# A four-layer convolution network on one core: the lead-in before the first matmul rebuilt

**Chip, cores, metric.** One core of a Trainium2 chip (trn2). The metric is device time in microseconds (us) of one execution, from the runs of one kernel on one chip; all runs quoted here are in the fast state (with one core no slower state showed: the granted clocks of the profiled runs lie between 0.952 and 0.955). Engines: PE (TensorE), DVE (VectorE), ACT (ScalarE), POOL (GpSimd), SP (SyncE, which issues most transfers).

## The reference

Four residual layers on x of 8192 samples x 8 channels x 16 x 16, float32. Each adds a layer of the group-normalized activations:

```python
x = x + L0(_gn(x))   # tensor-train matvec, cores of rank [1, 8, 8, 1], sizes [8, 16, 16], plus bias
x = x + L1(_gn(x))   # 3x3 convolution, batch norm over the whole batch, relu
x = x + L2(_gn(x))   # 3x3 convolution of values and weights quantized to +-127 (maximum over everything)
x = x + L3(_gn(x))   # 3x3 convolution with binarized weights, edge padding
```

`_gn` subtracts the mean and multiplies by 1/sqrt(var + eps) of each of four groups of channels of each sample. Batch norm and the global maximum force three passes over the 64 tiles of 128 samples (1 MiB each): pass 1 does layer 0 and the convolution of layer 1; pass 2 the batch norm and the maximum; pass 3 layers 2 and 3.

## The kernel before

First the constants, in program order (cut; every `by_channel` is 8 small transfers issued by SP):

```python
core2 = ...; for k in range(8): nc.sync.dma_start(core2[k * W:(k + 1) * W, k % 2], c2)
c0x = by_channel(c0, R * C, "c0x", setup)
for m0 in range(C): nc.sync.dma_start(c1x[m0 * H:(m0 + 1) * H], c1)
for r in range(R):                       # product of the first two cores, on DVE
    nc.vector.tensor_tensor(tmp, a, b, ALU.mult)          # 128x1024
    nc.vector.tensor_tensor(c01v, c01v, tmp, ALU.add)     # 128x1024, from r = 1
band1 = band(by_channel(w1, ...)); band2 = ...; band3 = ...   # five 128x384 operations each, DVE
# ... selectors, and kps = a small PE product for layer 3's correction
```

Then tiles 0 and 1 are loaded and normalized one after the other, and only then the main loop starts:

```python
for t in range(min(2, NT)):
    load_b(t); load_t(t); add_bias(t)         # xb: a copy in another layout, for the statistics
    norm_b_square(t)                          # ACT
    norm_b_sums(t)                            # DVE, four 128x1024 reductions
    norm_b_stats(t)                           # PE matmul into stb; DVE; POOL: power -0.5 of 64 columns
    norm_b_copy(t)                            # ACT: the power back into stb
    norm_b_apply(t)                           # DVE: xn = (xb - stb) * stb
expand(0, 0, 0); expand(0, 0, 1)              # PE pu, ACT copies it to u
for t in range(NT + 2):
    for q in range(NQ):                       # quarters of a tile
        # steps at r = 0..7, between the eight matmuls of main(t, q):
        at(2, ..., expand, next quarter, 0); at(6, ..., expand, next quarter, 1)
        # q == 0: at(4, norm_b_square, t + 2)
        # q == 1: at(0, norm_b_sums, t + 2);  at(7, norm_b_stats, t + 2)
        # q == 3: at(5, norm_b_copy, t + 2);  at(5, norm_b_apply, t + 2)
        main(t, q, steps)                     # PE: po, 8 matmuls of core01 with u (16 passes)
        conv_at(n, conv1)                     # PE: pc, an earlier tile
```

The PSUM tile `stb` has one buffer. Within an engine's stream the order of the program counts: in the kernel before, ACT's first copy of u (93.27 us) came only behind tile 1's copy into stb (93.11), though the pu that it reads had run at 81.52.

## Time and profile before

| | kernel before |
|---|---|
| median (range) of the runs beside the changed kernel | 4810.09 us (4809.37 to 4810.17, 4 runs) |
| span of the profiled run, granted clock | 4808.3 us, 0.955 |
| first po (the first matmul of the main work) | 99.26 us |
| end of pass 1 (SP issues the first load of pass 2) | 3217.39 us |
| PE busy | 92% |

Two marks carry the argument: the start of the first po, before which nothing of the main work is done, and the first load of pass 2, which SP issues when pass 1 is done.

### The profile page before, as it was taken

The numbers are of one execution on the slowest core, as the hardware profiler recorded it, in microseconds if no ns is written. First come the engines' busy times: TensorE is split into PE (matmuls) and PEld (weight loads), VectorE is DVE, ScalarE is ACT, GpSimd is POOL, SyncE is SP. The second block draws the span as 40 slices with busy tenths as digits, with TensorE's granted clock in tenths as the row PEclk, the third lists the DMA queues.
The fourth block names the chain that finished last, engine by engine and source line by source line (L and its number), as shares of the span: only waits on it lengthen the run. The fifth ranks groups of instructions, "written<-read, shape, count | busy, mean of one in ns | idle before, by whom it ended". The sixth has DMA issues, their size and how long they took to land. (4 is left out here: it accounts for less than half of the span.)

```text
span 4808.3 us, 47928 instructions
## 1 busy us (share of the span) xinstructions
PE 4409.3 (92%) x19338; PEld 1989.7 (41%) x19338; DVE 2689.6 (56%) x4058; ACT 2192.8 (46%) x1537; POOL 2009.3 (42%) x657
## 2 busy tenths in 40 slices
PE   2999999999999999999999999975555599999999
PEld 1444444444444444444444444431111244444444
DVE  4555555555555555545455555438888555665665
ACT  1444444444444444444444444434444455555553
POOL 3333333333332323242424232216666455556564
PEclk9999999999999999999999999986666799999999
DMA  2222221212222222222222222139997033333321
GB/s 90 79 79 97 79 97 75 101 70 100 76 95 81 89 87 88 88 88 88 88 88 88 88 88 79 53 138 398 382 383 307 18 140 131 132 140 132 132 104 79
DMA packets 82669, 581.16 MB, mean 121 GB/s; under 512 B 11536, under 2 KB 11664, under 8 KB 12048
## 3 DMA queue, kind: packets, MB, share of 16 engines
q1 hardware_dynamic: 82448, 578.10, 31.5%
q8 instruction: 153, 2.51, 0.2%
q14 instruction: 68, 0.56, 0.0%
HBM read 323.25 MB, written 254.80 MB: 120 GB/s over the span
## 5 line engine op out<-in xcount | busy, mean ns | idle before, releaser
L41 PE MATMUL po<-u,core 128*128 128x512 f32 x4096 | 1963.8, 607 | 2.2 <-ACT u L41 2.0
L41 ACT COPY u<-pu 128x2048 f32<-128x2048 f32 x512 | 955.8, 1867 | 1088.2 <-PE pu L41 1088.2
L41 PEld LDWEIGHTS po<-u,core 128*128 128x128 f32 x4096 | 721.6, 190 | 809.7 <-issue 802.9
L41 POOL TENSOR_TENSOR mv<-mv,mhalf 128x4 f32<-128x4 f32 x128 | 130.7, 1021 | 1790.5 <-DVE mv L41 1790.5
L41 POOL TENSOR_TENSOR mvb<-mvb,mhalf 128x64 f32<-128x64 f32 x64 | 675.1, 10549 | 164.7 <-DVE mvb L41 164.7
L41 PE MATMUL pc<-x1n,band 128*128 128x480 f32 (+1 forms) x1536 | 677.7, 578 | 4.0 <-DVE x1n L41 4.0
L41 PE MATMUL pf<-t,band 128*128 128x512 f32 x1536 | 676.0, 596 | 0.0
L41 PE MATMUL pu<-core,xn 32*128 32x256 f32 x8192 | 589.4, 402 | 11.6 <-ACT u L41 11.6
L41 PEld LDWEIGHTS pu<-core,xn 32*128 32x128 f32 x8192 | 371.3, 185 | 411.6 <-issue 386.7
L41 DVE BATCH_NORM_STATS2 bst<-y 128x6 f32<-128x512 f32 x256 | 177.7, 694 | 633.8 <-ACT y L41 633.8
L41 ACT ACTIVATE sq<-x 128x2048 f32<-128x2048 f32 x192 | 366.2, 1907 | 266.8 <-POOL x L41 266.1
L41 ACT ACTIVATE y<-pc,b 128x512 f32<-128x512 f32 x256 | 176.2, 688 | 663.0 <-PE pc L41 663.0
L41 PEld LDWEIGHTS pf<-t,band 128*128 128x128 f32 x1536 | 285.2, 189 | 390.6 <-issue 390.6
L41 DVE TENSOR_TENSOR x<-po,x 128x512 f32<-128x512 f32 x256 | 176.6, 690 | 482.5 <-PE po L41 240.4
L41 PEld LDWEIGHTS pc<-x1n,band 128*128 128x128 f32 x1536 | 293.3, 191 | 359.2 <-issue 359.2
L41 POOL TENSOR_TENSOR x<-x,z 128x1024 f32<-128x1024 f32 x128 | 299.8, 2365 | 185.2 <-ACT z L41 185.2
L41 POOL TENSOR_TENSOR x<-x,bias_t 128x2048 f32<-128x2048 f32 x64 | 289.4, 4521 | 181.7 <-DMA x<-in_xt 170.4
L41 POOL TENSOR_TENSOR x<-x,c 128x2048 f32<-128x2048 f32 x64 | 235.8, 3685 | 232.9 <-DVE t L41 221.9
L41 POOL TENSOR_TENSOR x<-x,yl 128x2048 f32<-128x2048 f32 x64 | 290.4, 4538 | 10.7 <-DMA x<-x_d 10.3
L41 PE MATMUL gb<-rows_c,sel 128*128 128x128 f32 x256 | 72.7, 436 | 237.3 <-DVE rows_c L41 237.3
L41 DVE TENSOR_TENSOR xn<-xb,stb 128x1024 f32<-128x1024 f32 x128 | 150.6, 1218 | 239.0 <-ACT stb L41 239.0
L41 DVE TENSOR_TENSOR x<-pf,x 128x1024 f32<-128x1024 f32 x128 | 156.4, 1222 | 116.1 <-PE pf L41 111.9
(161 smaller groups left out, 4027.7 us busy)
## 6 DMA issues: line engine op xcount, KB each, us to landing
x_d<-x SPq DMA_DIRECT2D x115, 1024.0 KB, 5.8
x<-x_d SPq DMA_DIRECT2D x115, 1024.0 KB, 8.3
xb<-in_xb SPq DMA_DIRECT2D x64, 1024.0 KB, 4.9
x<-in_xt SPq DMA_DIRECT2D x64, 1024.0 KB, 4.8
y_d<-y SPq DMA_DIRECT2D x64, 1024.0 KB, 3.8
yl<-y_d SPq DMA_DIRECT2D x64, 1024.0 KB, 11.4
out_dram<-x SPq DMA_DIRECT2D x64, 1024.0 KB, 3.9
c1x<-in_c SPq DMA_DIRECT2D x8, 64.0 KB, 2.2
```

Of the source, the lines that this page charges most:

```text
L41: return self.tc.keep_in_program_order(op(*args, **kwargs))
```

## The change

The intent is to start the main loop as early as tile 0 allows. The weights come in two transfers packed on the host, the product of the first two cores is done on PE, tile 0's power, copy and normalization go by quarters, tile 1's normalization moves into tile 0's main loop, and the other constants are built in slices between the first quarters. To make room, u has 2 buffers instead of 3 and yl of pass 2 has 4 instead of 5.

```diff
+PACK0 = [("c0", R * C), ("c1", R * H), ("core2", 2 * R * W), ("bias0", W)]
+PACK1 = [("w1", 9 * C), ("linb", C), ... ("w3all", C * C * 9), ("bias3", 1)]
+    w0 = load_pack(pack0, PACK0, const, "w0")          # one transfer on ACT's queue
+    def late_constants(late):                          # a generator: band1, band2, band3, selectors ...
+        w = load_pack(pack1, PACK1, late, "w1")
+        yield "load"
+        ...                                            # six more slices of DVE work, each with a yield
-        up = s.enter_context(tc.tile_pool(name="up", bufs=3))
+        up = s.enter_context(tc.tile_pool(name="up", bufs=2))
-            pool.tensor_tensor(mv[:, 1], mv[:, 1], mhalf[:, :NB], ALU.pow)
+            n = NB // NQ if by_quarter else NB
+            for a in range(0, NB, n):
+                pool.tensor_tensor(mv[:, 1, a:a + n], mv[:, 1, a:a + n], mhalf[:, :n], ALU.pow)
-        for t in range(min(2, NT)):
-            load_b(t) ... norm_b_apply(t)
-        expand(0, 0, 0)
-        expand(0, 0, 1)
+        for t in range(min(3, NT)):
+            load_b(t)
+            load_t(t)
+        rest = late_constants(...)
+        next(rest)
+        dve.tensor_tensor(c0x, w0["c0"]..., shz..., ALU.mult)
+        for n in range(C):
+            pe.matmul(cps[:, n], c0x[:, n]..., w0["c1"], start=True, stop=True)
+        norm_b_square(0)
+        ...  act.copy(core01, cps) in two halves
+        norm_b_sums(0)
+        norm_b_stats(0, by_quarter=True)
+        for q in range(NQ):
+            norm_b_copy(0, q)
+            norm_b_apply(0, q)
+            if q == 0:
+                expand(0, 0, 0)
+                expand(0, 0, 1)
+                add_bias(0)
         for t in range(NT + 2):
             for q in range(NQ):
+                if n > 0:
+                    next(rest, None)                   # one slice of constants
+                if t == 0 and NT > 1:
+                    if q == 0:
+                        at(0, True, norm_b_square, 1)
+                        at(0, True, norm_b_sums, 1)
+                        at(7, True, norm_b_stats, 1)
+                    elif q == 1:
+                        at(5, True, add_bias, 1)
+                        at(5, True, norm_b_copy, 1)
+                        at(5, True, norm_b_apply, 1)
+                        at(5, NT > 2, add_bias, 2)
-    with tc.tile_pool(name="p2", bufs=5) as p2, ...
+    with tc.tile_pool(name="p2", bufs=4) as p2, ...    # and kps moves here
```

## The prediction

> **What bounds the kernel now.** I read the page first, its row of PE over the span in 40 slices, then the stages with the windows view. In the windows rows the columns are the stretch and its length, then busy time and count of PE, PEld, DVE, ACT and POOL, the granted clock, the DMA share and GB/s.
>
> ```profile
> PE   2999999999999999999999999975555599999999
> 0.00:47.95 47.95, 1.65 (x6) 1.35 (x6) 31.89 (x71) 0.00 (x0) 1.75 (x15) 1.00 0.14 28
> 47.95:99.26 51.31, 5.68 (x37) 3.45 (x37) 20.26 (x23) 9.13 (x7) 34.64 (x5) 1.00 0.46 179
> 99.26:3214.00 3114.74, 3105.19 (x14302) 1452.36 (x14302) 1588.42 (x1965) 1363.17 (x954) 1020.31 (x251) 1.00 0.22 84
> 3214.00:3775.00 561.00, 291.09 (x1285) 95.24 (x1286) 446.36 (x854) 253.74 (x130) 354.39 (x130) 0.65 0.86 336
> 3775.00:4808.00 1033.00, 1005.67 (x3710) 437.30 (x3708) 602.63 (x1146) 566.76 (x446) 598.22 (x256) 0.99 0.31 117
> ```
>
> From 99.26 to 3214 us PE is busy 3105 of 3115 us, so layers 0 and 1 end when PE has done its work: whatever lets PE begin earlier moves everything after it by as much, and whatever makes PE wait there costs its full length. Before 99.26 PE does almost nothing. That lead-in is 2.1% of the time and the only place where the change can gain. Its chain stands in the timeline (start, length, then the instructions; in brackets the idle time before them and what ended it):
>
> ```profile
> 47.95 0.35 SPq L290 DMA_DIRECT2D xb<-in_xb  x1
> 52.94 2.35 DVE L41 TENSOR_REDUCE sumb<-xb 128x32 f32<-128x1024 f32 x2 [4.70 <-DMA xb<-in_xb]
> 60.70 10.57 POOL L41 TENSOR_TENSOR mvb<-mvb,mhalf 128x64 f32<-128x64 f32 x1 [0.48 <-DVE mvb L41]
> 82.52 10.56 POOL L41 TENSOR_TENSOR mvb<-mvb,mhalf 128x64 f32<-128x64 f32 x1 [6.74 <-DVE mvb L41]
> 93.27 1.86 ACT L41 COPY u<-pu 128x2048 f32<-128x2048 f32 x1
> 99.26 3.78 PE L41 MATMUL po<-u,core 128*128 128x512 f32 x4 [1.99 <-ACT u L41]
> 104.93 3.70 PE L41 MATMUL po<-u,core 128*128 128x512 f32 x8
> 120.35 0.38 PE L41 MATMUL stb<-sumb,sum 128*128 128x128 f32 x2
> 3198.59 12.86 PE L41 MATMUL pc<-x1n,band 128*128 128x512 f32 x24 [4.01 <-DVE x1n L41]
> ```
>
> Three parts: 48 us of constants before the first tile is even requested (some 90 small transfers issued by SP, core products on DVE); 5 us for the tile; then 46 us in which tile 0 and tile 1 are normalized one after the other, with a POOL power of 10.6 us in each, and ACT, which executes in order, comes to tile 0's first copy of u only after tile 1's power (93.1).
>
> **What the Trainium skill says.** (1) "TensorE: Matmul & The Clock Gate", Part 1: PE runs at half rate after an idle window of about 3.4 us until about 3.4 us of activity. The trace agrees: the first four po passes take 0.95 us each, later ones 0.46, and after an idle gap of 4.01 us the 24 pc passes at 3198.59 take 0.54 each, against 0.44 when warm (six in 2.63 us at 170.30). (2) "DMA: Bandwidth & Descriptors", Issuing engines are not separate DMA queues: transfers issued by SP and ACT interleave on the same 16 engines, so the second queue saves issue time, not bandwidth. Here xb lands 4.99 us after its issue and the next 1 MiB 2.77 us later, 379 GB/s; two queues at once do not occur in this trace. (3) "GPSIMD Engine Reference", section 3.1: a POOL add of 2048 fp32 takes 4497 ns; the bias add takes 4.52 here. It gives no time for a power; that I take from the trace.
>
> **The change, part by part.**
>
> *Removed: the wait for constants.* xb, x of three tiles now go out on SP at once, and the packs (0.24 and 0.71 MB) on ACT. xb(0) was issued at 47.95; now about 0.7, where SP's first issue stood. It lands after 5.0 us, plus 0.6 for 0.24 MB of pack at 379 GB/s, plus a little of the second pack: L = 6.5, an estimate. DVE's setup before it is four small operations and one 128x1024 product of 1.22 us; PE's product is 8 fp32 matmuls of 128 columns, 16 passes at 0.28 us (kps: six in 1.65), 4.4 us, done near 11 before the statistics ask for PE.
>
> *Tile 0.* From the landing to the start of the power: 60.70 - 52.94 = 7.8 us as before, so 14.2; less about 1.2 because the table load of 1.28 us no longer stands behind the tile, so 13.0. A power of 64 columns costs 10.55, one of 4 costs 1.02: 0.16 per column, so 16 columns take 2.9: 16.0. ACT copy 0.3; two DVE operations of 512 columns, 0.69 each (x<-po is of that size), 17.9. Then expand: pu 2.1, u 1.9, pu 2.1, u 1.9 (the cold pu's of 81.52 and 95.18), 26.0. First po at 26.0 instead of 99.26: **73.2 us saved.**
>
> *Tile 0's other quarters.* The program's waits chain ACT copy, two DVE operations, next copy, 1.75 us a quarter, after u at 26.0: quarter 1 is ready at 27.8 and PE asks at 29.8 (two cold po's, 3.8). No stall.
>
> *What is given back.* Tile 1's normalization moves into tile 0's main loop, tile 2's right after it. The small PSUM tile of the statistics (stb) has one buffer. In the built program the stb matmul of tile 2, in PE's stream in quarter 1, waits for the last DVE operation of tile 1's normalization, which reads that buffer. From stb(1) on: 120.35 to 121.66 (power starts) is 1.3; power 10.6; ACT copy 0.3; four DVE operations 4.7 (136.40 to 141.02 and a little): 17.0 us. PE has one quarter of work between the two, 9.7 us (x<-po at 111.72, 121.63, 131.16). So PE stands **17.0 - 9.7 = 7.3 us** at about 47 us. That is over 3.4 us, so it goes cold again: the first quarter took 12.4 (99.26 to 111.72) instead of 9.7, so **2.7 us** more.
>
> *Other constants on DVE between tiles.* Bands (five of 0.55 each), weights and selectors, some 20 us in all, in seven slices of 2.5 to 4 us. DVE is busy 51% in this stage. Following DVE's and ACT's order to tile 1 quarter 2, each thing PE asks for is there, with the closest at st(0), about 87, which DVE reaches with 0 to 1 us to spare: allow **1 us**.
>
> *Moved to the second pass:* kps, six passes and one subtraction, falls where PE and DVE wait for the first load (12.6 us idle of ACT at 3212 to 3225): 0. up from 3 to 2 buffers: u(n+1) replaces u(n-1), which PE finished before it started pu(n+1): 0. p2 from 5 to 4 buffers: yl's load then waits for POOL's add four tiles before; SP issues it after the store of a tile whose add ended about 1 us earlier (add 3261.76 to 3266.3, store 3267.5), and the load still has about three tile periods of 8.2 us against the 11.4 us it takes: 0.
>
> Sum: -73.2 + 7.3 + 2.7 + 1 = -62.2; 4810.1 - 62.2 = **4748 us**, 1.3% less.
>
> **Rivals.**
> - *The whole lead-in is kept:* if stb(2) didn't hold PE up, the gain is 72 to 73, 4737. For it: the wait is on an engine that is rarely late elsewhere. Against: the wait is in the program and 17.0 against 9.7 leaves little room.
> - *DVE becomes the bound of the first tiles:* 20 us of constants on top of two tiles' normalization. DVE executes in order, so a slice ahead of the evacuation of po or the statistics delays PE. If a third of it shows, 7 us more: 4755. For it: the small margin at st(0). Against: 51% busy and one pass.
> - *The smaller yl ring makes the second pass slower:* that pass moves 375 GB/s at a DMA share of 0.96 in 3222 to 3720, so it has little slack. Half a microsecond in each of 60 tiles would be 30: 4778. Against: ACT waited for yl 18.5 us in all, in 5 waits, all at the start; the tile's period is closed by DVE and POOL (power, rows, maximum, centring: 8.2 us).
> - *The first tile lands late:* six 1 MiB transfers and two packs at once. If the packs go first, 0.95 MB at 379 GB/s is 2.5 us: 2 us more, 4750.
>
> **Range and chances.** The gain's main term is the removal of a serial chain whose pieces are each measured; L and the cold starts are worth 3 us either way, the stall 4 (0 to 11), DVE up to 8. So 4748, 8 in 10 between 4738 and 4758. Faster by over 2% needs 4714 or less, 96 us, about the whole lead-in of 99: chance 0.01. Slower by over 2% needs a loss in each tile of a pass that nothing shows: 0.01. Within 2%: 0.98.
>
> **What would show it right or wrong.** The first po starts at 26 (24 to 30). Tile 0's first power lasts 2.9. One idle stretch of PE of about 7 us near 47 to 54 us, put down to DVE's xn or its own stb wait, then po passes near 0.9 us for about 5 us; no other PE wait over 2 us until the pass's end, which comes at about 3152 instead of 3214. The second pass still lasts 561 and the third 1033 within 3. It is wrong if the second pass is over 5 us longer (the buffers), if PE has no wait at stb (then about 4738), or if waits of several microseconds stand at st, po or pc in tiles 0 to 2 (DVE).

## The result and the profile after

| | before | after | difference |
|---|---|---|---|
| median (range), 4 runs each | 4810.09 (4809.37 to 4810.17) | 4746.35 (4745.77 to 4748.06) | -63.7 us |
| ratio, 95% interval | | 0.9868 [0.9851, 0.9886] | |
| span, granted clock | 4808.3, 0.955 | 4744.0, 0.953 | -64.3 |
| first po | 99.26 | 26.84 | -72.4 |
| end of pass 1 | 3217.39 | 3153.33 | -64.1 |
| first po to end of pass 1 | 3118.1 | 3126.5 | +8.4 |
| end of pass 1 to first pq (the first convolution of pass 3) | 557.3 | 557.1 | -0.3 |
| first pq to end of span | 1033.6 | 1033.6 | 0.0 |

The ratio is the mean time of one kernel's runs over that of the other's of the same rounds, so not quite the ratio of the medians.

The page's row of PE over 40 slices of the span, kernel after. Its first digit was 2 before: the empty lead-in filled most of the first slice of 120 us.

```profile
PE   7999999999999999999999999965555699999999
```

The marks, kernel before and then kernel after (the first po of before is in the prediction):

```profile
3217.39 0.32 SPq L557 DMA_DIRECT2D x<-x_d  x1
3774.72 2.72 PE L41 MATMUL pq<-q,band 128*128 128x512 bf16 x6 [6.59 <-ACT q L41]
```

```profile
3153.33 0.32 SPq L563 DMA_DIRECT2D x<-x_d  x1
3710.39 1.44 PE L41 MATMUL pq<-q,band 128*128 128x512 bf16 x3 [6.59 <-ACT q L41]
```

The windows view of the kernel after, from the start to the first po and from there to 3149.90, which is 64.1 us ahead of the edge that the prediction used (columns as there):

```profile
0.00:26.84 26.84, 8.76 (x51) 6.52 (x51) 9.05 (x15) 9.05 (x8) 14.67 (x20) 1.00 0.75 309
26.84:3149.90 3123.06, 3106.41 (x14304) 1452.99 (x14304) 1623.60 (x2036) 1364.57 (x959) 1043.32 (x255) 1.00 0.22 84
```

Passes 2 and 3 last as long as before, by the marks. Nearly the whole difference arose in the first 60 us, in the timeline of the kernel after (start, length, instructions; in brackets idle time and what ended it):

```profile
6.13 1.91 ACT L41 ACTIVATE sqb<-xb 128x2048 f32<-128x2048 f32 x1 [3.20 <-DMA xb<-in_xb]
6.38 1.23 DVE L41 TENSOR_TENSOR c0x<-w,shz 128x1024 f32<-128x1024 f32 x1 [3.39 <-DMA w<-in_pack]
7.53 2.34 DVE L41 TENSOR_REDUCE sumb<-xb 128x32 f32<-128x1024 f32 x2
...
13.97 11.54 POOL L41 TENSOR_TENSOR mvb<-mvb,mhalf 128x16 f32<-128x16 f32 x4 [11.34 <-DVE mvb L41]
18.70 2.09 PE L41 MATMUL pu<-w,xn 32*128 32x256 f32 x16 [5.72 <-DVE xn L41]
...
26.84 3.77 PE L41 MATMUL po<-u,core 128*128 128x512 f32 x4 [1.99 <-ACT u L41]
30.53 1.15 PE L41 MATMUL pu<-w,xn 32*128 32x256 f32 x16
...
37.28 0.38 PE L41 MATMUL stb<-sumb,sum 128*128 128x128 f32 x2
...
54.20 0.77 PE L41 MATMUL stb<-sumb,sum 128*128 128x128 f32 x2 [7.00 <-DVE xn L41]
54.76 4.24 PE L41 MATMUL po<-u,core 128*128 128x512 f32 x6
58.92 1.15 PE L41 MATMUL pu<-w,xn 32*128 32x256 f32 x16
```

Tile 0 (xb) and the first pack (w) land within 0.25 us of each other, near 6.1 and 6.4. The power goes in four pieces of 2.9 us, and the first piece is enough for quarter 0. The first po starts at 26.84. Then PE stands still for 7.00 us at the stb matmul of tile 2, which needs the one stb buffer that DVE's last xn operation of tile 1 still reads, and the six po passes after it take 4.24 us instead of 2.85 (37.50, kernel after): PE has gone cold, as this text calls passes at about half rate.

### The profile page after: what moved, and what is told of

Its sections match the earlier page's. It is cut to its first block, busy times and chain, and to the rows that moved or that the text cites. A ratio compares the mean times of both kernels' runs of the same rounds, so it can differ in the third digit from the quotient of the medians.

```text
span 4744.0 us, 47786 instructions
## 1 busy us (share of the span) xinstructions
PE 4410.5 (93%) x19292; PEld 1993.7 (42%) x19354; DVE 2681.9 (57%) x4051; ACT 2193.5 (46%) x1542; POOL 2010.7 (42%) x660
## 3 DMA queue, kind: packets, MB, share of 16 engines
q8 instruction: 153, 2.51, 0.2%
## 5 line engine op out<-in xcount | busy, mean ns | idle before, releaser
L41 POOL TENSOR_TENSOR mvb<-mvb,mhalf 128x64 f32<-128x64 f32 (+1 forms) x67 | 676.1, 10092 | 151.4 <-DVE mvb L41 151.4
L41 PE MATMUL pu<-w,xn 32*128 32x256 f32 x8192 | 588.5, 401 | 7.7 <-DVE xn L41 5.7
L41 PEld LDWEIGHTS pu<-w,xn 32*128 32x128 f32 x8192 | 370.9, 184 | 407.6 <-issue 391.9
L41 POOL TENSOR_TENSOR x<-x,w 128x2048 f32<-128x2048 f32 x64 | 289.6, 4526 | 131.8 <-DMA x<-in_xt 104.2
L41 DVE TENSOR_TENSOR xn<-xb,stb 128x1024 f32<-128x1024 f32 (+1 forms) x130 | 150.9, 1201 | 226.7 <-ACT stb L41 226.7
```

What stands on the lines that cost most here:

```text
L41: return self.tc.keep_in_program_order(op(*args, **kwargs))
```

## The experiments

Ten kernels were run, three or five rounds each, all correct. The table gives the marks of the profiled runs, which are the sharper measure: the totals carry some 2 us that come mostly from the start of pass 3 (below). The median of the kernel before was 4811.05, 4810.63 and 4810.33 in the three batches, for e1 to e4, e5 to e8, and e9 to e10.

| run | median, us (range) | ratio to before | first po | end of pass 1 | PE waits of over 1 us after the first po (to 140 us) |
|---|---|---|---|---|---|
| (after) | 4746.35 (4745.77 to 4748.06) | 0.9868 | 26.84 | 3153.33 | stb 7.00 |
| e1_stats_late | 4744.32 (4743.34 to 4745.5) | 0.9861 | 26.87 | 3149.98 | po 3.19, stb 1.46 |
| e2_stats_consts_late | 4744.0 (4738.43 to 4745.07) | 0.9858 | 26.64 | 3149.47 | po 3.19 |
| e3_consts_first | 4766.19 (4765.63 to 4766.7) | 0.9907 | 47.05 | 3172.99 | stb 6.99 |
| e4_tile0_whole | 4755.5 (4754.67 to 4756.98) | 0.9885 | 36.65 | 3162.66 | stb 7.00 |
| e5_copy_late | 4738.26 (4736.25 to 4738.67) | 0.9848 | 26.84 | 3143.70 | none |
| e6_warm | 4746.22 (4744.8 to 4746.79) | 0.9865 | 26.56 | 3154.15 | stb 7.00 |
| e7_dve_product | 4765.17 (4764.28 to 4765.91) | 0.9905 | 44.94 | 3172.82 | stb 7.00 |
| e8_before_rings | 4810.54 (4810.04 to 4811.14) | 0.9999 | 99.39 | 3217.88 | none |
| e9_warm_longer | 4734.09 (4733.13 to 4734.83) | 0.9842 | 24.69 | 3141.24 | none |
| e10_warm_pool_c0x | 4733.33 (4732.63 to 4734.86) | 0.9841 | 23.69 | 3139.86 | none |

### Where the gain comes from: e3, e4, e7

Each puts one part of the change back. e3 builds all other constants before tile 0:

```diff
-        next(rest)
+        for _ in rest:
+            pass
```

> Edit: all other constants are made on DVE ahead of tile 0, from the same packed transfer; the rest of the changed kernel stays. They are some 19 us of DVE work in its trace. If deferring them is a part of the gain by itself, the first po comes about 19 us later, at 46, and the time is 4765. If the packed transfers alone were the gain and DVE had room before tile 0 landed, the first po moves by under 5 us: 4746 to 4751.

Measured: 4766.19, first po at 47.05, 20.2 us later; the stall at stb stays as it was. In the timeline of e3:

```profile
10.71 0.15 DVE L41 COPY gamma<-w 128x1 f32<-128x1 f32 x1 [7.44 <-DMA w<-in_pack]
...
26.61 1.22 DVE L41 TENSOR_TENSOR c0x<-w,shz 128x1024 f32<-128x1024 f32 x1
...
47.05 3.59 PE L41 MATMUL po<-u,core 128*128 128x512 f32 x4 [1.99 <-ACT u L41]
```

So the 20.2 us are 15.9 us of DVE work (10.71 to 26.61) and 4.3 us of waiting: DVE now needs the second pack first, which lands at 10.71, where the first landed at 6.38 in the kernel after. The expectation named 19 us of work alone; its number came out by another sum. Hardly any of the gain from putting the constants off comes back as waits later: from the first po to the end of pass 1 it is 3125.9 us in e3 and 3126.5 in the kernel after.

e4 normalizes tile 0 in one piece:

```diff
-        norm_b_stats(0, by_quarter=True)
-        for q in range(NQ):
-            norm_b_copy(0, q)
-            norm_b_apply(0, q)
-            if q == 0:
-                expand(0, 0, 0); expand(0, 0, 1); add_bias(0)
+        norm_b_stats(0)
+        norm_b_copy(0)
+        norm_b_apply(0)
+        expand(0, 0, 0); expand(0, 0, 1); add_bias(0)
```

> Edit: tile 0 is normalized whole, not by quarters. The power takes 10.55 us instead of 2.93 for the first quarter, and the normalization 4.7 instead of 1.4: first po 10.9 us later, 37.8, time 4757, if the quarters act as the prediction had it. If the quarters only move the wait (their chain of copies delays tile 1, and the wait at stb shrinks by as much without them), under 4 us: 4750 or less.

Measured: 4755.5. In e4's timeline PE waits 15.48 us for the first pu where the kernel after waits 5.72, and the first po comes 9.8 us later. That is 1.1 less than expected: DVE's last operation on xn is two halves from 27.15, and pu starts after the first of them:

```profile
28.51 2.09 PE L41 MATMUL pu<-w,xn 32*128 32x256 f32 x16 [15.48 <-DVE xn L41]
...
36.65 3.50 PE L41 MATMUL po<-u,core 128*128 128x512 f32 x4 [1.99 <-ACT u L41]
```

e7 puts the product of the cores back on DVE, from the pack (its c1 is now repeated by the host, 0.46 MB more):

```diff
-        dve.tensor_tensor(c0x, ...)
-        for n in range(C):
-            pe.matmul(cps[:, n], c0x[:, n]..., w0["c1"], start=True, stop=True)
+        for r in range(R):                             # 8 multiplications and 7 additions, 128x1024
+            dve.tensor_tensor(c01v if r == 0 else tmp, a, b, ALU.mult)
+            if r: dve.tensor_tensor(c01v, c01v, tmp, ALU.add)
```

> The changed kernel with the product of the first two cores on DVE again, as in the kernel before (15 operations of 1024 columns), from the packed weights, ahead of tile 0's sums. The prediction's step (the product on PE lies beside the wait for tile 0) priced at its reverse: 15 operations of 1.1 to 1.2 us on DVE, less the 1.23 of c0x, stand ahead of the sums of tile 0: first po 15 to 17 us later, near 42 to 43, total near 4762. Rival (most of the gain is the packed transfer, and DVE would have been idle anyway): total within 4 us of the changed kernel.

Measured: 4765.17, first po 18.1 us later, a little more than expected. The timeline of e7 shows why:

```profile
7.81 1.22 DVE L41 TENSOR_TENSOR core<-w 128x1024 f32<-128x1024 f32 x1 [4.54 <-DMA w<-in_pack]
...
25.72 2.34 DVE L41 TENSOR_REDUCE sumb<-xb 128x32 f32<-128x1024 f32 x2
```

The product takes 25.72 - 7.81 = 17.9 us where c0x took 7.53 - 6.38 = 1.15, so 16.8 us; the other 1.4 is the larger pack, which lands at 7.81 instead of 6.38, and which the expectation had left out. The product on PE is thus worth 16.8 us.

Quarters (9.8), constants (20.2) and product (16.8) make 46.8, but they are not shares of the 72.4 us by which the first po moved: each is the price of putting one part back into the kernel after, the 20.2 hold a wait for the pack, and no run put two parts back together. What replacing the some 90 small transfers and taking tile 1 from ahead of tile 0 are worth was not measured.

### Where 8.4 us went: e1, e2, e5

The kernel after loses 8.4 us again between the first po and the end of pass 1. e1 moves tile 2's statistics from quarter 1 of tile 0 to the end of quarter 2, when tile 1's normalization has left stb:

```diff
+                    elif q == 2:                       # t == 0
+                        at(7, NT > 2, norm_b_stats, 2)
+                if t == 1 and q == 0 and NT > 2:
+                    at(5, True, norm_b_copy, 2)
+                    at(5, True, norm_b_apply, 2)
-                    at(7, ahead, norm_b_stats, t + 2)
+                    at(7, ahead and t > 0, norm_b_stats, t + 2)       # the copy and apply of q == 3 likewise
```

> Edit: only the place of tile 2's statistics is moved: its stb matmul from tile 0's quarter 1 to its quarter 2, its copy and normalization from tile 0's quarter 3 to tile 1's quarter 0. Theory A (what was given back is PE's wait for the single stb buffer, and the cold passes after it): the wait of 7.0 us and some 1.7 us of slow passes go, and nothing else rises: 4746.4 - 8.7 = 4737.7. Rival B (the wait only hid that DVE, with the constants between the tiles, is the bound of the first two tiles): PE waits elsewhere instead, for tile 3's sums, about 3.5 us or more, and the gain is 2 to 5 us: 4741 to 4744.

Measured: the wait of 7.00 us is gone, but the pass ends only 3.3 us earlier. e2 also moves all constants but the first slice to tiles 3 and later:

```diff
-                if n > 0:
+                if n == 1 or t >= 3 and q == 2:
                     next(rest, None)
```

> Edit: as the run before, and the constants that only the second and third pass use (all but those of layer 1) are made one slice per tile from tile 3 on, instead of one per quarter from tile 0 on. Theory A: the same as the run before, 4737.7, as DVE was never late. Rival B: the new wait for DVE of the run before goes, and only this run shows the whole 8.7 us: 4738, several microseconds below the run before.

Measured: 3.9 us earlier than after. Neither theory of the two expectations holds. e1's timeline has a wait on DVE with constants in front of the sums, of 1.46 us and not 3.5, and e2's has not; but both have a new wait of 3.19 us at po, which neither theory named. (e2 gains only 0.5 us on e1 because its clock rose later: from the first po to the eight po passes after it took 5.73 us in e2 and 4.69 in e1, with the same instructions.) First e1, then e2:

```profile
51.20 3.47 PE L41 MATMUL po<-u,core 128*128 128x512 f32 x4 [3.19 <-ACT u L41]
92.33 0.49 PE L41 MATMUL stb<-sumb,sum 128*128 128x128 f32 x2 [1.46 <-DVE sumb L41]
```

```profile
50.05 0.22 ACT L41 COPY stb<-mvb 128x64 f32<-128x64 f32 x1 [5.82 <-POOL mvb L41]
50.20 1.86 ACT L41 COPY u<-pu 128x2048 f32<-128x2048 f32 x1
...
52.11 2.83 PE L41 MATMUL po<-u,core 128*128 128x512 f32 x4 [3.19 <-ACT u L41]
```

ACT stood idle for 5.82 us on POOL's power of tile 1, because the small copy into stb (norm_b_copy(1), step 5 of quarter 1) stands in its order ahead of the second copy of u for quarter 2. PE needs that u. In the kernel after this wait is there as well, but hidden: ACT's copy of stb is at 49.19 and u at 49.34 there, while PE waits for stb until 54.20 anyway. e5 is e2 with this copy, and the two DVE operations after it, moved too (shown against e2):

```diff
                     elif q == 1:                       # t == 0
-                        at(5, True, norm_b_copy, 1)
-                        at(5, True, norm_b_apply, 1)
+                    elif q == 2:
+                        at(0, True, norm_b_copy, 1)
+                        at(0, True, norm_b_apply, 1)
```

> The version with tile 2's statistics and the constants late, and tile 1's copy into the small PSUM tile (with the two DVE operations after it) also moved, from step 5 of tile 0's quarter 1 to the start of quarter 2, so that it no longer stands in ACT's order ahead of quarter 2's second copy of u. Theory (the 8.4 us that the pass still loses after the first po are nothing but this order of the first tiles' small steps): no PE wait of 1 us or more after the first po, the pass ends 8 to 9 us earlier than in the changed kernel, near 3145, total 4737 to 4739. Rival (another engine is the bound by then, so that each wait removed brings up the next): a wait of 3 us or more stands somewhere in tiles 0 to 2, and the pass ends near 3150 as in the two runs before, total 4743 to 4745.

Measured: 4738.26, the pass ends 9.6 us earlier than after. e5's timeline has PE lines without brackets at the places of both waits:

```profile
45.96 4.04 PE L41 MATMUL po<-u,core 128*128 128x512 f32 x8
...
56.68 0.38 PE L41 MATMUL stb<-sumb,sum 128*128 128x128 f32 x2
```

So all of the 8.4 us can be had back by putting small steps of the first tiles elsewhere: there were two waits, one behind the other, and the cold passes after them. e5 has the constants late as well, so a kernel with the two moves alone was not run; e1's wait of 1.46 us is a sign that DVE with the constants would hold PE up a little.

### The half-rate start: e6, e9, e10

The first two pu and four po passes run at half rate. e6 fills the gaps ahead of them with matmuls that nobody reads:

```diff
         norm_b_stats(0, by_quarter=True)
+        idle = ps_m.tile([P, BANK], F32, name="idle", tag="mm")
+        def warm(n):
+            for _ in range(n):
+                pe.matmul(idle[:, 0:256], ident, c0x[:, 0:2]..., start=True, stop=True)
+        warm(5)                                        # e9: 12
...
                 expand(0, 0, 0)
+                warm(1)                                # e9: 2
                 expand(0, 0, 1)
+                warm(1)                                # e9: 2
```

> The changed kernel with eleven idle matmuls less four, that is seven of 256 columns whose result nobody reads: five after tile 0's statistics, where PE waits 5.7 us for xn, and one after each of the first two pu. Theory (the first pu and po run at half rate only because PE stood idle before them): pu takes 1.15 instead of 2.09 twice, the first four po passes 1.86 instead of 3.77, so the first po starts at 25.0 and the first quarter ends 3.8 us earlier; the 7.0 us wait for tile 2's statistics remains as it is, since it hangs on DVE and POOL, which start from PE's stb of tile 1 and so move along. Pass 1 ends 3 to 4 us earlier, near 3150, total 4742 to 4743. Rival (the low rate there is not from idleness but belongs to the first some 30 us): po still 3.77 and the total 4746.

Measured: nothing gained, 4746.22, and po still 3.78. The failure is one of size, and its timeline says so:

```profile
12.54 2.32 PE L41 MATMUL idle<-c0x,ident 128*128 128x256 f32 x10
18.42 2.09 PE L41 MATMUL pu<-w,xn 32*128 32x256 f32 x16 [3.56 <-DVE xn L41]
...
26.56 3.78 PE L41 MATMUL po<-u,core 128*128 128x512 f32 x4 [0.83 <-ACT u L41]
```

PE was warm at 12.54 (10 passes of 256 columns in 2.32 us, 0.23 each), so the fill lasted about half as long as ten cold passes would have (an estimate: 0.47 us each, half of a cold po pass, which has twice the columns), and the 3.56 us left were enough to make it cold. The granted clock of the windows view shows the same: in e6 it is 1.00 until 17 us and 0.50 from 18 to 30. (In the kernel after this view reads 1.00 from 18 to 32 although the passes run at half rate; the lengths of the passes are the surer sign.) e9 is e5 with twelve of them, and two at the later places:

> The version without any PE wait after the first po (statistics, constants and copy late), plus idle matmuls again, now sized from the run that failed: there five of them lasted only 2.32 us and left PE idle for 3.56 us before the first pu, long enough to go cold. Now twelve after tile 0's statistics (12 x 0.464 = 5.6 us of the 5.7 us) and two after each of the first two pu. Theory (PE runs at half rate there only because of the idle gap before): pu 1.15 instead of 2.09 twice, first four po passes 1.86 instead of 3.77, first po at 25.0 instead of 26.84, end of pass 1 some 3.8 us earlier than without (near 3140), total 4734 to 4735. Rival (the rate is low in the first 30 us whatever PE does): pu 2.09, po 3.77, total 4738.

```profile
12.55 5.35 PE L41 MATMUL idle<-c0x,ident 128*128 128x256 f32 x24
18.43 1.15 PE L41 MATMUL pu<-w,xn 32*128 32x256 f32 x16 [0.54 <-DVE xn L41]
...
24.69 1.98 PE L41 MATMUL po<-u,core 128*128 128x512 f32 x4 [0.93 <-ACT u L41]
```

Now pu takes 1.15 and the four po passes 1.98, and the granted clock is 1.00 from 8 to 32 us. The first po is 2.15 us earlier than in e5, as expected, but the end of pass 1 only 2.5 us instead of 3.8: PE, being faster, waits 0.44 us for ACT's u at 31.81 and 0.16 for DVE at 34.17. In the steady part of the pass the lead is 2.9 us (the batch norm sums of one quarter start at 172.44 in e5 and 169.55 in e9); at its end the last 24 pc passes took 13.11 us in e9 and 11.77 in e5. The total is 4734.09. So half rate costs this lead-in 2.5 to 2.9 us. The Trainium skill's page "TensorE: Matmul & The Clock Gate", Part 1, warns of idle gaps of PE over about 3.4 us. Here 3.56 us (e6) did make PE cold, but so did a shorter gap of 3.19 us (e1, e2; e1's four po passes at 51.20 took 0.87 each). After 0.93 us (e9) and 1.46 us (e1, po passes of 0.47 at 92.65) it stayed warm.

e10 takes c0x off DVE, and puts tile 0's statistics in the middle of the core product in PE's order; eight idle matmuls follow instead of twelve:

```diff
-        dve.tensor_tensor(c0x, ...)
+        pool.tensor_tensor(c0x, ...)
...
+            if n == C // 2:
+                norm_b_stats(0, by_quarter=True)
             pe.matmul(cps[:, n], ...)
```

> The same, with the one large DVE operation ahead of tile 0's sums (c0x, 1.23 us) on POOL, which idles then, and tile 0's statistics in PE's order after half of the core product instead of all of it. Theory (DVE's c0x stands in the lead-in's chain; the tile lands at 6.1 and the sums start at 7.5): sums, stb, power and first po 1.2 to 1.4 us earlier, first po near 23.7, total about 1.3 us less than the version without it. Rival (POOL takes 2.3 us and more for c0x, so PE's product and its two copies on ACT hold up the first copy of u): first po no earlier, total the same or more.

Measured: POOL takes 2.00 us for c0x, DVE's sums start at 6.28 instead of 7.58, the first po at 23.69 instead of 24.69 (1.0 us), and pass 1 ends 1.4 us earlier. The totals, 4733.33 and 4734.09, overlap and don't tell the two apart. e9 and e10 are the fastest kernels found; both beat the kernel before and the kernel after.

### The buffers: e8

e8 is the kernel before with two u buffers and four yl buffers.

```diff
-        up = s.enter_context(tc.tile_pool(name="up", bufs=3))
+        up = s.enter_context(tc.tile_pool(name="up", bufs=2))
-    with tc.tile_pool(name="p2", bufs=5) as p2, ...
+    with tc.tile_pool(name="p2", bufs=4) as p2, ...
```

> The kernel before with the two buffer counts of the changed one and nothing else: two u buffers instead of three, four yl buffers instead of five. The prediction's step says 0 for both: total within 1.5 us of the kernel before, second pass 561 within 1 us. Rival (the smaller rings cost something that the changed kernel hides in its lead-in or second pass): 5 us or more slower, with waits of ACT for yl in the second pass or of PE for u in the first.

Measured: 4810.54 against 4810.63, ratio 0.9999 [0.9985, 1.0014]; ACT's waits for yl in pass 2 sum to 17.7 us (18.5 before). From the end of pass 1 to the first pq it took 557.2 us (557.3 before). The smaller rings cost nothing that these runs show.

### What blurs the totals

e1 and e2 ended pass 1 3.3 and 3.9 us earlier than after, but their totals are only 2.0 and 2.4 us lower. The difference arises at the start of pass 3, where PE works in short bursts between waits. The second group of pq matmuls, kernel after, and then e1:

```profile
3713.33 1.51 PE L41 MATMUL pq<-q,band 128*128 128x512 bf16 x6
```

```profile
3710.76 2.73 PE L41 MATMUL pq<-q,band 128*128 128x512 bf16 x6
```

Over the profiled runs this group took 1.46 (before), 1.51 (after), 2.73 (e1), 2.51 (e2), 1.67, 1.74, 2.33, 1.55, 1.52 (e3 to e7), 1.56 (e8), 1.74 and 2.43 (e9, e10). From the first pq to the end of the span it took 1035.2 to 1035.9 us in the four with over 2 us (e1, e2, e5, e10) and 1033.6 to 1034.3 in the others. The granted clock in the stretch of this group was 0.93 in the kernel after (3713 to 3716) and 0.51 in e1 (3710.4 to 3713.4). The same code runs there in all of them; why the clock rises sooner in some was not tested. A total thus says nothing about differences below some 2 us. The marks of pass 1 do.

## Why the prediction was right, step by step

- **Time.** 4748 predicted, 8 in 10 between 4738 and 4758; 4746.35 measured. Its sum was -62.2, the medians give -63.7. In part two errors cancelled: the first po came 0.8 us later than said, and 2.6 us less were given back, 0.9 of them by chance (below).
- **First po at 26.0: 26.84.** From the start of the power to the first po it took 12.9 us for the predicted 13.0, with 2.9 us of power, 1.73 us a quarter (ACT's copies of stb at 26.68, 28.41, 30.14) and the cold pu as listed. The power started at 13.97 instead of 13.0. The step that was off is the one that put c0x beside the wait for tile 0: the pack landed 0.25 us after xb, so c0x ran until 7.53, ahead of the sums. e10 shows it: with c0x off DVE the power starts 1.0 us earlier (12.72 against 13.71 in e9).
- **The wait at stb, 7.3: 7.00**, at 54.20 rather than at the "about 47" where it begins (47.20); put down to DVE's xn, as said. e1 removes it by moving the statistics.
- **Cold after it, 2.7: 1.7.** This term was mis-sized: from the stb matmul to the next pu it took 4.72 us (54.20 to 58.92) instead of 3.00 (37.28 to 40.28). The estimate took the whole loss of the first quarter, where PE was cold up to 104.93, 5.7 us; after the stall it was warm again by 58.92, 4.7 us. The first quarter itself also became warm sooner than before (its pu took 1.15 instead of 2.03), 0.9 us gained that no step had. That was luck: from the first po to the eight po passes after it took 4.77 us here and 5.67 before, but 5.73 in e2 with the same instructions.
- **DVE's constants, 1: 0.2** (st, 86.61). The work was put at some 20 us; undisturbed it is 15.9 (e3), and in the kernel after one band operation takes 4.77 us beside POOL's add (69.57) instead of 0.56. The order was as close as said: in e1, where the statistics of tile 2 come later, DVE's constants do hold PE up, by 1.46.
- **Sum of what is given back: 11 predicted, 8.4 measured** (7.0 + 1.7 + 0.2 - 0.9 = 8.0; 0.4 not attributed).
- **Rings and kps, 0: 0**, by the marks of the kernel after (557.1 and 1033.6, for 557.3 and 1033.6 before) and, for the rings, in e8.
- **The rivals.** "The whole lead-in is kept" named 4737 if stb(2) didn't hold PE up. That price was too good for that one wait: e1 took it away and gained 3.3 us of the pass, since the copy of stb in ACT's order was next. This second wait the prediction did not see; it had "each thing PE asks for is there". Its price was reached, 4738.26, only with both moved and the constants late (e5). "DVE becomes the bound" fell (0.2 us), "the smaller yl ring" fell (e8), "the first tile lands late" fell (6.1).

## What to carry to other kernels

Before a pass that one engine fills, each microsecond until that engine's first instruction counts nearly in full (in e3 the first po came 20.2 us later and pass 1 ended 19.7 us later), and work that it doesn't need yet (here 16 us of constants) can go beside it at almost no cost. After such a move, look in the timeline for the small steps of the first tiles that an in-order engine meets too early: a wait may hide a second one just behind it, so read what the other engines stand at before pricing its removal. Judge changes of a few microseconds by marks in the trace, since the clock of a half-idle stage elsewhere can blur totals by as much.

## What the Trainium skill lacked or had wrong

- "GPSIMD Engine Reference", section 3.1, gives an add but no power. On POOL a power of float32 took 10.56 us for 64 columns, 2.9 us for 16 and 1.01 to 1.02 us for 4.
- "SBUF — State Buffer", Who interferes with whom, says that a DVE instruction with two SBUF inputs contends with a GpSimd instruction that reads SBUF, and calls the ports that they share an exclusive lock. For POOL's add the trace of the kernel after agrees: the small product mvb at 55.33 took 2.88 instead of 0.23 us and ended with POOL's add, while xn operations with one operand in PSUM ran through an add at 1.2 us each. For the power it doesn't: the two-input operation at 40.98 took 0.56 us, as in e3 with POOL idle (12.47), in the middle of one that reads SBUF too. No run tested this by itself, and how long the power holds the ports is open. From the timeline of the kernel after:

```profile
38.59 10.56 POOL L41 TENSOR_TENSOR mvb<-mvb,mhalf 128x64 f32<-128x64 f32 x1 [8.60 <-DVE mvb L41]
49.12 9.01 POOL L41 TENSOR_TENSOR x<-x,w 128x2048 f32<-128x2048 f32 x2
...
40.98 0.56 DVE L41 TENSOR_TENSOR acc<-acc,tmp 128x384 f32<-128x384 f32 x1
51.70 2.35 DVE L41 TENSOR_TENSOR xn<-xn,stb 128x1024 f32<-128x1024 f32 x2
55.33 2.88 DVE L41 TENSOR_TENSOR mvb<-mvb 128x64 f32<-128x64 f32 x1
```
